# An attention and mixture-of-experts layer in float32: its products in two of 64 stationary columns each, and the scores' masked quarter left out

## The chip, the cores and the metric

The kernel runs on one core of a Trainium2 chip. The metric is the device time of one execution in microseconds (us); lower is better. Engines are named as in the profile: PE is TensorE's matmuls, PEld its weight loads, DVE is VectorE, ACT ScalarE, POOL GpSimd, SP the sync engine, whose queue issues nearly all DMA transfers.

## What is computed

The input is normalised, and three things are added to it: a linear attention with decay (32 heads of 128, 2 sequences of 512 tokens), and a base layer with eight low-rank experts, of which two are taken for each token. The attention is

```
qkv = silu(hidden_states @ qkv_w.T)
...
def step(kv, blk):
    cq, ck, cv = blk
    scores = jnp.einsum('bhnd,bhmd->bhnm', cq, ck) * diag_decay
    intra = jnp.einsum('bhnm,bhmd->bhnd', scores, cv)
    inter = jnp.einsum('bhnd,bhde->bhne', cq * q_decay, kv)
    kv_next = kv * block_decay + jnp.einsum('bhnd,bhne->bhde', ck * k_decay, cv)
    return (kv_next, intra + inter)
...
xf = xf * jax.lax.rsqrt(jnp.mean(xf * xf, axis=-1, keepdims=True) + EPS)
normed = norm_w * xf
gate = jax.nn.sigmoid(hidden_states @ gate_w.T)
return gate * normed @ out_w.T
```

`diag_decay` is zero where a key is later than the query, so within a block the scores are needed only where the key is not later. The reference uses blocks of 32 tokens; the kernel uses blocks of 128, which gives the same sum.

## The kernel before

Everything is float32. A product of a 128x128 stationary operand with N moving columns is one `nc.tensor.matmul` in the code, and two loads and two matmul records (here called passes) in the trace.

**Projections.** The products with the weights of v, gate, q and k are done by a fast scheme with seven products instead of eight, used twice, one inside the other. The list `rounds` has one entry for each outer product of each of 16 sets of weights; a round has seven slots (`SLOTS`), one for each inner product (`inner_product`, two products of 256 moving columns; L431 where tokens are stationary, which gives v, and L434 where the weights are). GpSimd forms the weights' sums two rounds ahead (`encode`, L162 to L187). `after` takes the results from PSUM with ScalarE and VectorE and adds them up. Sets 0 to 7 give v and gate, which go to DRAM; sets 8 to 15 give q and k of four heads each, which stay in SBUF.

**Attention.** As soon as q and k of one head and sequence (an item, 64 in all) are there, `attend` runs on it, in steps that are spread over the slots of later rounds by `stages` and `later`:

- v comes back from DRAM (L660).
- k's first three blocks are transposed: VectorE turns 32x32 squares (L665), a trip through DRAM puts the squares in their places (L668, then four transfers at L673) as `kt`.
- scores: four products of 128 keys (stationary) by 128 queries (L678), into one PSUM bank; VectorE multiplies them by the decays within a block (L680, `mask[:, 0]`), with keys on the partitions, into `sc`.
- GpSimd multiplies q by the decay from the block's start (L683, `mask[:, 1]`), the gate comes from DRAM (L686).
- ScalarE scales `kt` by each key's decay to the block's end into `kd` (L690), a column of the mask.
- three products of `kd` and v (L696), from which VectorE forms the running states (L698, L700).
- seven products (L706, L708) give the attention's output, transposed; VectorE multiplies it by the gate (L710), ScalarE squares it (L717), GpSimd adds the squares up (L718), and it goes to DRAM (L720).

`load_mask` (L446, L447) fetches an item's decays when the first part of its q and k is placed, four buffers in all: a 128x128 table with the keys on the partitions, and one row of 128 for the queries, given to all partitions.

**The rest.** The setup normalises x and transposes it on TensorE (L264, with an identity matrix), and runs the router and part of the base layer's products (L314). The output projection (`out_product`, L806) is again in seven products of 256 columns and begins before the attention ends.

**Order.** The order on PE, ACT, DVE, POOL and SP is the one in which the code issues the instructions (`tc.manual_schedule`). `mm` is a helper, so in the trace all its products have line 90. The tile tags tell them apart: `ps_sc<-qk` scores, `ps_sc<-v,kd` keys by values, `ps_at<-scores,v` and `ps_at<-qd,state` the output.

The "scores" ring has three buffers of 128x512. Before the attention it also serves the base layer's results and the experts' weights and biases.

Of the kernel before, what the change touches and what calls it, by code (L numbers as in the profile page):

```python
# [35 lines left out]
F32 = mybir.dt.float32  # L36
# [6 lines left out]
P = 128  # L43
# [18 lines left out]
def attn_moe_kernel(ctx: ExitStack, tc: tile.TileContext, x, qk_w, v_w, gate_w, out_w, norm_w,  # L62
# [22 lines left out]
    def ring(tag, shape=None):  # L85
        n, bufs = RING[tag]
        return work.tile(shape or [P, n * 512], F32, tag=tag, name=tag, bufs=bufs)

    def mm(o, lhsT, rhs, start, stop):
        nc.tensor.matmul(o, lhsT, rhs, start=start, stop=stop)  # L90

    ssq = [keep.tile([P, S], F32, tag=f"ssq{b}", name=f"ssq{b}") for b in range(B)]
    ident = keep.tile([P, P], F32, tag="ident", name="ident")
    nw = keep.tile([P, H], F32, tag="nw", name="nw")

    g_kept = [dram.tile([P, 2, 2, B, S // 2], F32, tag=f"g_kept{p}", name=f"g_kept{p}") for p in range(NP)]
# [108 lines left out]
    with tc.tile_pool(name="setup", bufs=1, side="right") as sp:  # L205
        x_sb = [sp.tile([P, HID], F32, tag=f"x{t}", name=f"x{t}") for t in range(NT)]
        nc.gpsimd.memset(eps, EPS)

        halves = (slice(0, HID // 2), slice(HID // 2, HID))
        for queue, of in zip((nc.sync, nc.scalar), halves):  # L210
# [76 lines left out]
        def base():  # L287

            pa, pb = seeded[:2], first_banks
            pc, pd, y, w = {}, {}, {}, {}  # L290

            def done(b, half, h, o):
                nc.sync.dma_start(x_base[:, TB * b + 2 * h : TB * b + 2 * h + 2, half * HO : (half + 1) * HO],
                                  o.rearrange("p (t n) -> p t n", t=2))

            def copied(tag, t):
                o = ring(tag, [P, 512])
                nc.scalar.copy(o, t)
                return o

            def added(t, u):
                o = ring("scores")
                nc.vector.tensor_tensor(o, t, u, ALU.add)
                return o


            units = [(1, 0, 0), (1, 0, 1), (2, 0, 0), (2, 0, 1), (1, 1, 0), (1, 1, 1), (2, 1, 0), (2, 1, 1)]
            for q, h, i in units + [(q, h, i) for q in (5, 6, 7, 3, 4) for h in range(2) for i in range(2)]:
                if q == 5 and i == 0:
                    pc[h] = bank("sc")  # L310
                t = {1: pa, 2: pa, 5: pc, 3: pc, 6: pb, 7: pd, 4: pd}[q][h]
                of = slice((2 * h + i) * P, (2 * h + i + 1) * P)
                for c in range(2):
                    nc.tensor.matmul(t[:, i * HO : (i + 1) * HO], xo[q][:, c, of], wo[q][:, c, :],  # L314
                                     start=q in (1, 5) and i == 0 and c == 0, stop=True, skip_group_check=True)
                if i == 0:
                    pass
                elif q == 1:
                    nc.scalar.copy(pb[h], t)
                elif q == 2:  # L320
                    done(0, 0, h, copied("scores", t))
                elif q == 5:
                    y[h] = copied("gT", t)
                elif q == 6:
                    pd[h] = pa[h]
                    nc.scalar.copy(pd[h], t)
                    w[h] = copied("gate", t)
                elif q == 7:
                    done(1, 1, h, added(t, y[h]))
                elif q == 3:  # L330
                    done(1, 0, h, added(t, w[h]))
                else:
                    done(0, 1, h, copied("scores", t))
                yield
# [16 lines left out]
        for g, ts in enumerate(groups):  # L351
            rstd = inv_sqrt(*roots[g])
            xns = []
            for i, t in enumerate(ts):
                xn = ring("gate")
                for of in halves if t == 0 else (slice(0, HID),):
                    (nc.vector if t < NT - 1 else nc.gpsimd).tensor_scalar(
                        xn[:, of], x_sb[t][:, of], mv[:, t, 0:1], rstd[:, i : i + 1], ALU.subtract, ALU.mult)
                xns.append(xn)

            for t in range(2 * g, 2 * g + 2) if 0 < g < 4 else ():
                statistics(t)
            for t, xn in zip(ts, xns):
                transpose(t, xn)
                for what in AFTER[t]:
                    if what == "base":
                        next(chunks)
                    else:
                        router(what)
        nc.vector.tensor_tensor(wsums[0], a21, a22, ALU.add)  # L370
        nc.vector.tensor_tensor(wsums[1], wsums[0], a11, ALU.subtract)
        nc.vector.tensor_tensor(wsums[2], a11, a21, ALU.subtract)
# [50 lines left out]
    def inner_product(o, r, i, first):  # L423
        n, q = rounds[r]
        a = operand[n, q][i]
        x_ = {1: xo[q][:, 0, :HB], 2: xo[q][:, 1, :HB], 3: xo[q][:, 1, HB:], 4: xt[q - 1][:, 3],
              5: xt[q - 1][:, 0], 6: xt[q - 1][:, 1], 7: xt[q - 1][:, 2]}[i]
        for u in range(2):
            if kind(n) == 0:

                nc.tensor.matmul(o.rearrange("p (g j d) -> p j g d", g=2, j=2)[:, u], x_[:, u * P : (u + 1) * P],  # L431
                                 a, start=first and u == 0, stop=True, skip_group_check=True)
            else:
                nc.tensor.matmul(o[:, u * HB : (u + 1) * HB], a[:, u], x_, start=first and u == 0, stop=True,  # L434
                                 skip_group_check=True)

# [3 lines left out]

    def load_mask(head):

        mask = work.tile([P, 2, P], F32, tag="mask", name="mask", bufs=4)
        nc.sync.dma_start(mask[:, 0, :], decay[head][:, :P])  # L446
        nc.sync.dma_start(mask[:, 1, :], decay[head][P - 1, P : 2 * P].partition_broadcast(P))  # L447
        return mask

    spare = cycle(5 * ["v"] + 2 * ["gT"])  # L450

# [202 lines left out]
    def attend(head, b):  # L654
# [7 lines left out]


        squares = work.tile([P, 4, TB - 1, 32], F32, tag="squares", name="squares", bufs=2)
        nc.vector.transpose(squares.rearrange("p c j d -> p j c d"), k[:, : (TB - 1) * P])  # L665
        yield
        kept = dram.tile([P, 4, TB - 1, 32], F32, tag="k_kept", name="k_kept", bufs=3)
        nc.sync.dma_start(kept, squares)  # L668
# [6 lines left out]

        pc = bank("sc")
        for j in range(TB):
            mm(pc[:, j * P : (j + 1) * P], k[:, j * P : (j + 1) * P], q[:, j * P : (j + 1) * P], True, True)  # L678
        sc = ring("scores", [P, TB, P])
        nc.vector.tensor_tensor(sc, pc.rearrange("p (j n) -> p j n", j=TB),  # L680
                                mask[:, 0, :].unsqueeze(1).to_broadcast([P, TB, P]), ALU.mult)
        qd = work.tile([P, TB - 1, P], F32, tag="qd", name="qd", bufs=3)
        nc.gpsimd.tensor_tensor(qd, q[:, P:].rearrange("p (j n) -> p j n", j=TB - 1),  # L683
                                mask[:, 1, :].unsqueeze(1).to_broadcast([P, TB - 1, P]), ALU.mult)
        gate = ring("gate")
        nc.sync.dma_start(gate, gate_kept[s_][:, u, f, b, :])  # L686
        yield

        kd = work.tile([P, TB - 1, P], F32, tag="kd", name="kd", bufs=2)
        nc.scalar.activation(kd.rearrange("p j (a d) -> p a j d", a=4), kt, AF.Copy,  # L690
                             scale=mask[:, 0, P - 1 : P])
        yield

        pu = bank("sc")
# [8 lines left out]
        pa = bank("at")  # L703
        for j in range(TB):
            o = pa[:, j * P : (j + 1) * P]
            mm(o, v[:, j * P : (j + 1) * P], sc[:, j, :], True, j == 0)  # L706
            if j:
                mm(o, state[:, j - 1, :], qd[:, j - 1, :], False, True)  # L708
        gT = ring("gT")
# [84 lines left out]
    def out_product(f, p, n, sums, only=None):  # L794

        a, w = gated[f, p], w_o[p]
        o = sums[n] if isinstance(sums[n], list) else [sums[n][:, i * HO : (i + 1) * HO] for i in range(2)]
        if n in (1, 2):
            l, r = a[:, n - 1, 0], w[:, n - 1, :HO]
        else:  # L800
            s, t = gsum[f, p], wsum[f, p]
            l, r = {3: (s[:, 3], w[:, 1, HO:]), 4: (a[:, 1, 1], t[:, 3]), 5: (s[:, 0], t[:, 0]),
                    6: (s[:, 1], t[:, 1]), 7: (s[:, 2], t[:, 2])}[n]
        for i in range(2):
            if only in (None, i):
                nc.tensor.matmul(o[i], l[:, i * P : (i + 1) * P], r,  # L806
                                 start=p == 0 and (i == 0 or isinstance(sums[n], list)), stop=p == NP - 1, skip_group_check=True)

    EARLY = 4
    sums = [{}, {}]  # L810
# [36 lines left out]
    for k in range(7 * len(rounds) + 7):  # L847
        now[0] = k
        r0, m = divmod(k, 7)
        if m == 0:  # L850
            if r0 == 3:
                routing = route()
            if r0 == 15:
                for slots, g in zip((2, 5, 11, 18), 4 * [transpose_experts()]):
                    later[k + slots].append(g)
            if r0 in range(18, 18 + 3 * NT, 3):
                for slots, g in zip((0, 8, 11, 13), 4 * [experts((r0 - 18) // 3)]):
                    later[k + slots].append(g)
# [257 lines left out]
```

## Time and profile before

| | us |
|---|---|
| median of 3 runs | 1130.0 (1128.63 to 1130.0) |
| span of the profiled execution | 1129.5 |
| granted TensorE clock | 1.00 throughout |
| DMA moved | 198.24 MB in 192254 packets, 176 GB/s |

The costliest groups of the attention and of the projections, by line, with busy time and the mean of one:

| line | what | count | busy us | mean ns |
|---|---|---|---|---|
| L434 | PE, `sd<-xt,e`, 256 columns (the largest such group) | 672 | 172.6 | 379 |
| L90 | PE, scores, 128 columns | 512 | 67.5 | 275 |
| L90 | PE, `kd` by v, 128 columns | 384 | 53.6 | 276 |
| L90 | PE, output from scores, 128 columns | 512 | 88.4 | 275 |
| L90 | PE, output from states, 128 columns | 384 | 74.2 | 275 |
| L680 | DVE, scores by decays, 128x512 | 64 | 43.9 | 686 |
| L665 | DVE, transposes of k, 128x384 | 64 | 35.6 | 566 |
| L690 | ACT, `kd`, 128x384 | 64 | 39.1 | 612 |
| L698 | DVE, copy from PSUM, 128x128 | 64 | 18.3 | 286 |
| L276 | ACT, copy from PSUM, 128x136 | 8 | 2.2 | 272 |

Matmuls are pipelined and their ends are modelled, so the mean of a PE record (379 ns) is longer than the distance from one to the next; the distance is read from the chain of waits in order of time, where a row is a start, a duration, and how many records follow each other. A count of PE records is a count of passes, two for each product. `SPq` is the queue of the sync engine; a row of a tile's view gives shortest, median and longest duration in ns, and then the first and last start in us.

### The profile page before, as it was taken

What the parts mean: (1) busy time and instruction counts of PE and PEld (TensorE: products, weight loads), DVE (VectorE), ACT (ScalarE), POOL (GpSimd) and SP (SyncE); (2) the same over time, 40 slices, a digit from 0 to 9 for tenths busy, and PEclk for the clock granted to TensorE, in tenths of its full rate; (3) what the DMA queues carried; (4) which work ended last, traced back from release to release, by engine and by line L of the source; (5) the groups of instructions that cost most, each with busy time, mean ns of one, the idle gap of its engine ahead of it and who ended that gap; (6) DMA issues with size and microseconds to landing.
All of it is one profiled execution on the core that took longest, in us unless ns stands there. A gap on an engine that the chain in (4) does not pass through costs nothing.

```text
span 1129.5 us, 18355 instructions
## 1 busy us (share of the span) xinstructions
PE 1120.4 (99%) x6064; PEld 1004.9 (89%) x6064; DVE 755.1 (67%) x1343; ACT 433.9 (38%) x778; POOL 763.5 (68%) x819
## 2 busy tenths in 40 slices
PE   8999999999999999999999999999999999999998
PEld 8888888888888888998999999999999998888887
DVE  7676766675665667776767767677777775545424
ACT  4344444444435434343343444435344442320000
POOL 3568778779768767666686866768776666554552
PEclk9999999999999999999999999999999999999999
DMA  5534574664553456666665766766666677943221
GB/s 169 161 112 158 168 235 157 193 203 156 186 168 122 159 146 198 168 195 187 208 193 173 209 170 179 204 190 198 179 186 174 200 229 242 329 162 118 90 92 56
DMA packets 192254, 198.24 MB, mean 176 GB/s; under 512 B 50976, under 2 KB 164384, under 8 KB 192032
## 3 DMA queue, kind: packets, MB, share of 16 engines
q1 hardware_dynamic: 192016, 196.94, 56.9%
q8 instruction: 49, 0.80, 0.3%
q14 instruction: 45, 0.37, 0.1%
q10 hardware_dynamic: 144, 0.13, 0.0%
HBM read 126.70 MB, written 70.30 MB: 174 GB/s over the span
## 4 chain that ended last, share of the span: by engine, by line
PE 93%; DMA 3%; DVE 2%; SPq 1%; issue 1%; POOL 1%; ACT 0%; ACTq 0%; DVEq 0%; POOLq 0%
PE ps_fr L434 20%; PE sd L434 18%; PE ps_at L90 9%; PE ps_sc L90 9%; PE sd L431 6%; PE sd L806 6%; PE ps_sc L806 5%; PE ps_fr L806 5%; PE ps_sc L434 4%; PE ps_sc L431 4%; PE ps_fr L431 4%; DMA k_kept<-squares 2%; PE ps_at L806 1%; PE sd L314 1%; DMA kt<-k_kept 1%; PE ps_sc L314 1%
## 5 line engine op out<-in xcount | busy, mean ns | idle before, releaser
L718 POOL TENSOR_TENSOR ssq<-ssq,sq 128x512 f32<-128x512 f32 x62 | 78.9, 1273 | 146.9 <-ACT sq L717 146.9
L434 PE MATMUL sd<-xt,e 128*128 128x256 f32 x672 | 172.6, 379 | 0.0
L483 ACT ACTIVATE qk<-qk 128x512 f32<-128x512 f32 x128 | 80.4, 630 | 207.0 <-DVE qk L506 206.9
L434 PEld LDWEIGHTS sd<-xt,e 128*128 128x128 f32 x672 | 123.6, 190 | 17.2 <-issue 2.6
L538 ACT COPY sd<-sd 128x512 f32<-128x512 f32 x112 | 64.1, 573 | 137.9 <-PE sd L434 69.3
L521 DVE TENSOR_TENSOR w<-sd,sum 128x512 f32<-128x512 f32 x110 | 74.5, 690 | 63.1 <-ACT sd L538 62.9
L527 ACT COPY sd<-ps_fr 128x512 f32<-128x512 f32 x112 | 64.2, 573 | 77.3 <-PE ps_fr L434 49.2
L90 PE MATMUL ps_at<-scores,v 128*128 128x128 f32 x512 | 88.4, 275 | 0.0
L787 POOL TENSOR_TENSOR wsum<-wo 128x256 f32<-128x256 f32 x48 | 39.2, 834 | 68.2 <-PE sd L806 28.9
L90 PEld LDWEIGHTS ps_at<-scores,v 128*128 128x128 f32 x512 | 77.4, 191 | 3.4
L786 DVE TENSOR_TENSOR gsum<-gated 128x256 f32<-128x256 f32 x54 | 25.9, 520 | 80.7 <-PE ps_sc L806 56.6
L162 POOL TENSOR_TENSOR s<-raw 128x1024 f32<-128x1024 f32 x32 | 75.6, 2364 | 5.0 <-DMA raw<-in_v_w 2.9
L90 PE MATMUL ps_at<-qd,state 128*128 128x128 f32 x384 | 74.2, 275 | 0.0
L434 PE MATMUL ps_fr<-xsum,s 128*128 128x256 f32 x288 | 74.0, 379 | 0.0
L710 DVE SCALAR_TENSOR_TENSOR gT<-gate,ps_at 128x512 f32<-128x512 f32 x64 | 43.6, 682 | 41.9 <-PE ps_at L90 36.8
L90 PEld LDWEIGHTS ps_sc<-qk 128*128 128x128 f32 x512 | 67.2, 192 | 3.3
L90 PE MATMUL ps_sc<-qk 128*128 128x128 f32 x512 | 67.5, 275 | 0.0
L181 POOL TENSOR_TENSOR e<-s 128x256 f32<-128x256 f32 x64 | 46.6, 728 | 28.7 <-PE sd L434 18.0
L683 POOL TENSOR_TENSOR qd<-qk,mask 128x384 f32<-128x384 f32 x64 | 64.3, 1005 | 2.4 <-PE ps_at L90 2.0
L680 DVE TENSOR_TENSOR scores<-ps_sc,mask 128x512 f32<-128x512 f32 x64 | 43.9, 686 | 22.4 <-PE ps_sc L90 20.0
L434 PEld LDWEIGHTS ps_fr<-xsum,s 128*128 128x128 f32 x288 | 53.1, 190 | 6.4
L90 PEld LDWEIGHTS ps_sc<-v,kd 128*128 128x128 f32 x384 | 52.6, 191 | 6.8 <-ACT kd L690 3.7
(345 smaller groups left out, 2905.8 us busy)
## 6 DMA issues: line engine op xcount, KB each, us to landing
raw<-in_qk_w SPq DMA_DIRECT2D x64, 256.0 KB, 4.3
v<-v_kept SPq DMA_DIRECT2D x64, 256.0 KB, 4.4
gate<-gate_kept SPq DMA_DIRECT2D x64, 256.0 KB, 3.3
g_kept<-gT SPq DMA_DIRECT2D x64, 256.0 KB, 3.3
gated<-g_kept SPq DMA_DIRECT2D x27, 512.0 KB, 3.8
k_kept<-squares SPq DMA_DIRECT2D x64, 192.0 KB, 3.5
kt<-k_kept SPq DMA_DIRECT2D x256, 48.0 KB, 2.1
gate_kept<-v SPq DMA_DIRECT2D x47, 256.0 KB, 2.5
```

What stands on the lines that cost most here:

```text
L90: nc.tensor.matmul(o, lhsT, rhs, start=start, stop=stop)
L162: nc.gpsimd.tensor_tensor(t, a, b, op)
L181: nc.gpsimd.tensor_tensor(e[:, 0], a21, a22, ALU.add)
L431: nc.tensor.matmul(o.rearrange("p (g j d) -> p j g d", g=2, j=2)[:, u], x_[:, u * P : (u + 1) * P], a, start=first and u == 0, stop=True, ...
L434: nc.tensor.matmul(o[:, u * HB : (u + 1) * HB], a[:, u], x_, start=first and u == 0, stop=True, skip_group_check=True)
L483: nc.scalar.activation(v, v, AF.Silu)
L521: nc.vector.tensor_tensor(o, v, t, ALU.add)
L527: nc.scalar.copy(st["pb"], st["pa"])
L538: nc.scalar.copy(st["pd"], st["pb"])
L683: nc.gpsimd.tensor_tensor(qd, q[:, P:].rearrange("p (j n) -> p j n", j=TB - 1), mask[:, 1, :].unsqueeze(1).to_broadcast([P, TB - 1, P]), A ...
L718: nc.gpsimd.tensor_tensor(ssq[b], ssq[b], sq, ALU.add)
L806: nc.tensor.matmul(o[i], l[:, i * P : (i + 1) * P], r, start=p == 0 and (i == 0 or isinstance(sums[n], list)), stop=p == NP - 1, skip_grou ...
```

## The change

A product in `mm`, once the setup's transposes are issued (`in_halves`), becomes two, each of 64 of the 128 stationary columns and all the moving columns; each writes its own 64 partitions of the result. `inner_product`, `out_product` and the base layer's products go through `mm` too. With `turned`, the two halves of the stationary columns change places in the result: this is done for the odd blocks of v, so that in an odd block tokens 64 to 127 stand on partitions 0 to 63.

The scores of a block become two products: the early 64 keys by all 128 queries, and the late 64 keys by the late 64 queries. The late keys by the early queries, which the decay makes zero, are no longer computed; their places in the three tiles of scores are set to zero once (`zero_scores`, at round 50), and the three tiles are then used in turn. In odd blocks the two products write the other half's partitions, as v's tokens stand there.

What follows from the order of the halves: the mask has five parts of 64 columns, loaded by five transfers (table and row, with halves exchanged for odd blocks). VectorE's multiplication of the scores becomes three instructions, one for the late queries of all blocks and two of 64 partitions for the early ones. The transposition of k becomes two, for the even blocks and for block 1, and the scaling to `kd` becomes two on ScalarE. The identity matrix moves to the setup's memory.

```diff
@@ -86,11 +86,20 @@
         n, bufs = RING[tag]
         return work.tile(shape or [P, n * 512], F32, tag=tag, name=tag, bufs=bufs)
-    def mm(o, lhsT, rhs, start, stop):
-        nc.tensor.matmul(o, lhsT, rhs, start=start, stop=stop)
+    HP = P // 2
+    in_halves = [False]
+    def mm(o, lhsT, rhs, start, stop, turned=0, **more):
+        if not in_halves[0]:
+            nc.tensor.matmul(o, lhsT, rhs, start=start, stop=stop, **more)
+            return
+        for h in range(2):
+            of = h ^ turned
+            nc.tensor.matmul(o[h * HP : (h + 1) * HP], lhsT[:, of * HP : (of + 1) * HP], rhs, start=start, stop=stop,
+                             **more)
     ssq = [keep.tile([P, S], F32, tag=f"ssq{b}", name=f"ssq{b}") for b in range(B)]
-    ident = keep.tile([P, P], F32, tag="ident", name="ident")
     nw = keep.tile([P, H], F32, tag="nw", name="nw")
     g_kept = [dram.tile([P, 2, 2, B, S // 2], F32, tag=f"g_kept{p}", name=f"g_kept{p}") for p in range(NP)]
@@ -205,6 +214,7 @@
     with tc.tile_pool(name="setup", bufs=1, side="right") as sp:
         x_sb = [sp.tile([P, HID], F32, tag=f"x{t}", name=f"x{t}") for t in range(NT)]
         nc.gpsimd.memset(eps, EPS)
+        ident = sp.tile([P, P], F32, tag="ident", name="ident")
         halves = (slice(0, HID // 2), slice(HID // 2, HID))
         for queue, of in zip((nc.sync, nc.scalar), halves):
@@ -311,8 +321,8 @@
                 t = {1: pa, 2: pa, 5: pc, 3: pc, 6: pb, 7: pd, 4: pd}[q][h]
                 of = slice((2 * h + i) * P, (2 * h + i + 1) * P)
                 for c in range(2):
-                    nc.tensor.matmul(t[:, i * HO : (i + 1) * HO], xo[q][:, c, of], wo[q][:, c, :],
-                                     start=q in (1, 5) and i == 0 and c == 0, stop=True, skip_group_check=True)
+                    mm(t[:, i * HO : (i + 1) * HO], xo[q][:, c, of], wo[q][:, c, :],
+                       q in (1, 5) and i == 0 and c == 0, True, skip_group_check=True)
                 if i == 0:
                     pass
                 elif q == 1:
@@ -367,6 +377,7 @@
                         next(chunks)
                     else:
                         router(what)
+        in_halves[0] = True
         nc.vector.tensor_tensor(wsums[0], a21, a22, ALU.add)
         nc.vector.tensor_tensor(wsums[1], wsums[0], a11, ALU.subtract)
         nc.vector.tensor_tensor(wsums[2], a11, a21, ALU.subtract)
@@ -428,11 +439,10 @@
         for u in range(2):
             if kind(n) == 0:
-                nc.tensor.matmul(o.rearrange("p (g j d) -> p j g d", g=2, j=2)[:, u], x_[:, u * P : (u + 1) * P],
-                                 a, start=first and u == 0, stop=True, skip_group_check=True)
+                mm(o.rearrange("p (g j d) -> p j g d", g=2, j=2)[:, u], x_[:, u * P : (u + 1) * P], a,
+                   first and u == 0, True, turned=u, skip_group_check=True)
             else:
-                nc.tensor.matmul(o[:, u * HB : (u + 1) * HB], a[:, u], x_, start=first and u == 0, stop=True,
-                                 skip_group_check=True)
+                mm(o[:, u * HB : (u + 1) * HB], a[:, u], x_, first and u == 0, True, skip_group_check=True)
@@ -442,10 +452,23 @@
     def load_mask(head):
-        mask = work.tile([P, 2, P], F32, tag="mask", name="mask", bufs=4)
-        nc.sync.dma_start(mask[:, 0, :], decay[head][:, :P])
-        nc.sync.dma_start(mask[:, 1, :], decay[head][P - 1, P : 2 * P].partition_broadcast(P))
+        mask = work.tile([P, 5, HP], F32, tag="mask", name="mask", bufs=4)
+        near = decay[head][:HP]
+        nc.sync.dma_start(mask[:HP, 0:2, :], near[:, :P])
+        nc.sync.dma_start(mask[:HP, 2, :], near[:, :HP])
+        nc.sync.dma_start(mask[HP:, 0, :], near[:, :HP])
+        nc.sync.dma_start(mask[HP:, 1:3, :], near[:, :P])
+        nc.sync.dma_start(mask[:, 3:5, :], decay[head][P - 1, P : 2 * P].partition_broadcast(P))
         return mask
+    score_tiles = []
+    def zero_scores():
+        for _ in range(RING["scores"][1]):
+            sc = ring("scores", [P, TB // 2, 2, 2, HP])
+            nc.gpsimd.memset(sc[HP:, :, 0, 0, :], 0.0)
+            nc.gpsimd.memset(sc[:HP, :, 1, 0, :], 0.0)
+            score_tiles.append(sc)
     spare = cycle(5 * ["v"] + 2 * ["gT"])
@@ -662,7 +685,10 @@
         squares = work.tile([P, 4, TB - 1, 32], F32, tag="squares", name="squares", bufs=2)
-        nc.vector.transpose(squares.rearrange("p c j d -> p j c d"), k[:, : (TB - 1) * P])
+        blocks_of_k = k.rearrange("p (j c d) -> p j c d", j=TB, d=32)
+        nc.vector.transpose(squares[:, :, 0::2].rearrange("p c j d -> p j c d"), blocks_of_k[:, 0 : TB - 1 : 2])
+        nc.vector.transpose(squares[:, :, 1].rearrange("p (h c) d -> p h c d", h=2)[:, ::-1],
+                            blocks_of_k[:, 1].rearrange("p (h c) d -> p h c d", h=2))
         yield
         kept = dram.tile([P, 4, TB - 1, 32], F32, tag="k_kept", name="k_kept", bufs=3)
         nc.sync.dma_start(kept, squares)
@@ -675,20 +701,32 @@
         pc = bank("sc")
         for j in range(TB):
-            mm(pc[:, j * P : (j + 1) * P], k[:, j * P : (j + 1) * P], q[:, j * P : (j + 1) * P], True, True)
-        sc = ring("scores", [P, TB, P])
-        nc.vector.tensor_tensor(sc, pc.rearrange("p (j n) -> p j n", j=TB),
-                                mask[:, 0, :].unsqueeze(1).to_broadcast([P, TB, P]), ALU.mult)
+            for late in range(2):
+                at, asked = late ^ (j % 2), slice(j * P + late * HP, (j + 1) * P)
+                keys = slice(j * P + late * HP, j * P + (late + 1) * HP)
+                nc.tensor.matmul(pc[at * HP : (at + 1) * HP, asked], k[:, keys], q[:, asked], start=True, stop=True,
+                                 skip_group_check=True)
+        sc = score_tiles[0]
+        score_tiles.append(score_tiles.pop(0))
+        scored = pc.rearrange("p (a r h n) -> p a r h n", a=TB // 2, r=2, h=2)
+        nc.vector.tensor_tensor(sc[:, :, :, 1], scored[:, :, :, 1],
+                                mask[:, 1:3].unsqueeze(1).to_broadcast([P, TB // 2, 2, HP]), ALU.mult)
+        for r in range(2):
+            of = slice(r * HP, (r + 1) * HP)
+            nc.vector.tensor_tensor(sc[of, :, r, 0], scored[of, :, r, 0],
+                                    mask[of, 0].unsqueeze(1).to_broadcast([HP, TB // 2, HP]), ALU.mult)
         qd = work.tile([P, TB - 1, P], F32, tag="qd", name="qd", bufs=3)
         nc.gpsimd.tensor_tensor(qd, q[:, P:].rearrange("p (j n) -> p j n", j=TB - 1),
-                                mask[:, 1, :].unsqueeze(1).to_broadcast([P, TB - 1, P]), ALU.mult)
+                                mask[:, 3:5].rearrange("p h n -> p (h n)").unsqueeze(1).to_broadcast([P, TB - 1, P]),
+                                ALU.mult)
         gate = ring("gate")
         nc.sync.dma_start(gate, gate_kept[s_][:, u, f, b, :])
         yield
         kd = work.tile([P, TB - 1, P], F32, tag="kd", name="kd", bufs=2)
-        nc.scalar.activation(kd.rearrange("p j (a d) -> p a j d", a=4), kt, AF.Copy,
-                             scale=mask[:, 0, P - 1 : P])
+        for r, js in enumerate((slice(0, TB - 1, 2), slice(1, 2))):
+            nc.scalar.activation(kd[:, js].rearrange("p j (a d) -> p a j d", a=4), kt[:, :, js], AF.Copy,
+                                 scale=mask[:, 1 + r, HP - 1 : HP])
         yield
         pu = bank("sc")
@@ -703,7 +741,7 @@
         pa = bank("at")
         for j in range(TB):
             o = pa[:, j * P : (j + 1) * P]
-            mm(o, v[:, j * P : (j + 1) * P], sc[:, j, :], True, j == 0)
+            mm(o, v[:, j * P : (j + 1) * P], sc[:, j // 2, j % 2].rearrange("p h n -> p (h n)"), True, j == 0)
             if j:
                 mm(o, state[:, j - 1, :], qd[:, j - 1, :], False, True)
         gT = ring("gT")
@@ -803,8 +841,8 @@
                     6: (s[:, 1], t[:, 1]), 7: (s[:, 2], t[:, 2])}[n]
         for i in range(2):
             if only in (None, i):
-                nc.tensor.matmul(o[i], l[:, i * P : (i + 1) * P], r,
-                                 start=p == 0 and (i == 0 or isinstance(sums[n], list)), stop=p == NP - 1, skip_group_check=True)
+                mm(o[i], l[:, i * P : (i + 1) * P], r, p == 0 and (i == 0 or isinstance(sums[n], list)), p == NP - 1,
+                   skip_group_check=True)
     EARLY = 4
     sums = [{}, {}]
@@ -853,6 +891,8 @@
             if r0 == 15:
                 for slots, g in zip((2, 5, 11, 18), 4 * [transpose_experts()]):
                     later[k + slots].append(g)
+            if r0 == 50:
+                zero_scores()
             if r0 in range(18, 18 + 3 * NT, 3):
                 for slots, g in zip((0, 8, 11, 13), 4 * [experts((r0 - 18) // 3)]):
                     later[k + slots].append(g)
```

## The prediction

> **What bounds the kernel now.** I read the page's totals first, then the table of stages, then the chain of waits in order of time.
>
> ```profile
> span 1129.5 us, 18355 instructions
> ## 1 busy us (share of the span) xinstructions
> PE 1120.4 (99%) x6064; PEld 1004.9 (89%) x6064; DVE 755.1 (67%) x1343; ACT 433.9 (38%) x778; POOL 763.5 (68%) x819
> ```
>
> TensorE fills 99% of the span, so a microsecond of its passes is a microsecond of time, unless something makes it wait. The attention items run from 400 to 940 us. There the stage table shows what room the others have:
>
> ```profile
> core 0: us, PE busy (x) PEld busy (x) DVE busy (x) ACT busy (x) POOL busy (x), PEclk, DMA share, GB/s
> 400.00:940.00 540.00, 538.29 (x3339) 495.89 (x3338) 393.27 (x720) 227.60 (x406) 377.96 (x387) 1.00 0.66 191
> ```
>
> TensorE misses 1.7 of 540 us at a granted clock of 1.00; VectorE is busy 73%. A busy record says little of what a pass costs; the chain gives its pace. Each float32 product stands there as two passes: the scores' four products as x8, the three of keys and values as x6, seven output products as x14.
>
> ```profile
> 646.05 0.89 PE ps_sc L90 x8
> 646.94 0.87 PE sd L434 x4
> 647.81 0.86 PE ps_fr L434 x4
> 648.67 0.67 PE ps_sc L90 x6
> 649.34 0.86 PE sd L434 x4
> 650.21 0.86 PE ps_fr L434 x4
> 651.07 1.56 PE ps_at L90 x14
> ```
>
> A pass of 128 moving columns costs 112 ns (0.89/8, 0.67/6, 1.56/14), one of 256 costs 216 ns (0.865/4). The timeline tells why 112 is over half of 216:
>
> ```profile
> 508.07 0.30 PEld L90 LDWEIGHTS ps_at<-qd,state 128*128 128x128 f32 x2
> 508.18 0.39 PE L90 MATMUL ps_at<-qd,state 128*128 128x128 f32 x2
> 508.30 0.73 PEld L434 LDWEIGHTS ps_fr<-xsum,raw 128*128 128x128 f32 x4
> 508.41 1.03 PE L434 MATMUL ps_fr<-xsum,raw 128*128 128x256 f32 x4
> ...
> 509.06 0.84 PEld L434 LDWEIGHTS ps_fr<-xt,e 128*128 128x128 f32 x4
> 509.27 1.03 PE L434 MATMUL ps_fr<-xt,e 128*128 128x256 f32 x4
> ```
>
> The weight load begins 0.11 us before its pass where passes have 128 columns, so load and pass are of one length there; beside 256 columns it has half the time to spare.
>
> **The sum, part by part.** It is made against the profiled execution, 1129.5 us, 0.5 below the median of the runs.
>
> *Scores.* An item has 8 passes of 128 columns: 8 x 112 = 896 ns. After, four blocks give 8 passes of 128 columns and 8 of 64, each on half of the stationary columns. If the two halves are worked side by side, each with its own order, the exchange in odd blocks gives either half 4 of 128 and 4 of 64. No row has 64 columns: half of 112 is 56, the line through 112 and 216 gives 60; I take 60, the dearer. 4 x 112 + 4 x 60 = 688, 208 ns saved, times 64 items: **-13.3 us**. Bounds: -14.3 (56 ns), and nothing.
>
> *All other products in two.* If the halves run beside each other, a slot of 216 or 112 ns carries two passes as it carried one, but two loads. If a load of 64 columns takes half of 112 ns, two take what one took: 0. If it took the whole 112, every slot would be at least 224: 1792 attention passes (64 x 28) lose 112 ns and the other 4272 lose 8, 201 + 34 = 235 us, the upper bound. Below: if loads of the two halves overlap, attention's passes come down to half of 216, 4 ns x 1792 = -7 us. I take **0**. The nearest fact is that one load fills 128 columns in 0.11 us; no row here loads fewer.
>
> The Trainium skill (TensorE: Matmul & The Clock Gate, "LDWEIGHTS") lets a load's time go with its columns; by that the zero stands. The trace, with 128 columns everywhere, cannot show it.
>
> *VectorE.* The scores' multiplication, 691 ns for 512 columns, becomes one of 256 and two of 128 on half the partitions. Copies from PSUM of 128 columns take 286 ns (L698); the line through 286 and 691 gives 421 for 256. 421 + 2 x 286 = 993, +0.30 us. The transposition of 384 columns (566 ns) becomes two; the same line's fixed part, 0.15 us, is paid once more. 64 x 0.45 = 29 us: 393 becomes 422 of 540, 78%. The cover is VectorE's own idle time; without it the 29 us would stand in the time.
>
> *ScalarE.* The scaling of kd (607 ns) in two: at most another 0.27 (the copy of 136 columns in setup, L276), 17 us on 228 of 540. Hidden. *GpSimd:* six memsets before the first item, each below the 0.73 us of a 128x256 operation: under 4.4 us, in a stage where it waits 2 to 4 us at a time for TensorE. Hidden. One switch to halves, the moved identity and the views: nothing.
>
> *SP's queue.* The mask comes in five transfers for two, 192 more on the one queue:
>
> ```profile
> L446 SPq DMA_DIRECT2D mask<-in_decay x64: 357/568/975, 403.3 to 922.6; - x64
> L447 SPq DMA_DIRECT2D mask<-in_decay x64: 333/448/1325, 404.0 to 923.2; - x64
> L673 SPq DMA_DIRECT2D kt<-k_kept x256: 302/424/1994, 411.1 to 935.9; - x128
> ```
>
> At 0.45 to 0.57 us that is 86 to 109 us of issuing. The stage now has some 704 issues (256 kt, 128 masks, 64 each of v, gate, g_kept, k_kept, q/k weights) at about 0.45: 317 of 540 us, 59%; then 75 to 79%. Behind the masks on that queue stand kt, v, gate, the stores and the next weights. What is late next is kt, then ScalarE's kd, then the products of keys and values:
>
> ```profile
>   DMA kt<-k_kept: 9.5, 5
> who waited for it (us, times):
>   ACT kd L690: 9.5, 5
>   PEld ps_sc L90: 3.7, 4
>   DVE gT L710: 2.3, 4
>   PE ps_sc L90: 2.2, 3
> ```
>
> TensorE and its loads lose up to 5.9 us on this path today. Bounds for the growth: 0 (the spare 40% of the queue takes it), and 86 us (all of it shows). As the queue keeps a fifth of its time, I take two thirds of today's loss again: **+4 us**, VectorE's later releases included.
>
> Sum: 1129.5 - 13.3 + 0 + 4 = 1120.2; with the half microsecond to the median, **1120.7 us**. Its own range: 1129.5 - 14.3 - 7 = 1108 to 1128 (gain as taken, three times the drag).
>
> **Rivals.** *Passes start strictly in order (slower).* The two passes of a product's first half come ahead of those of its second, so the second half then always lags by a pass. At equal lengths nothing is lost. But on going from 256 columns to 128, the first half is done while the other is still in its last long pass, and the next pass in the order belongs to that other half: one 128-column slot stays empty, 112 ns. The scores gain nothing either: a 64-column pass must wait its turn behind a 128-column pass of the other half, and two blocks take the eight slots that they took. The chain shows three such groups per item, each between 256-column products: 3 x 64 x 112 ns = 21.5 us, so 1129.5 + 21.5 + 4 = **1155**. It decides as soon as a pass that waits for its half holds back those behind it. For it: in the trace one pass follows another without exception. Against: with one tile of 128 columns nothing else could be seen, and TensorE does not work its records one by one (a load runs beside the pass ahead of it), so I give independent halves more than this.
>
> The Trainium skill speaks on both sides. TensorE: Matmul & The Clock Gate ("What overlaps and what doesn't") has matmuls in strict first-in, first-out order; TensorEngine Tiling (Array Packing) ("Key Properties") says that "Tiles operate independently". By the first the sum would be 1155, by the second 1121; no row of this case has two tiles.
>
> *SP or VectorE becomes late (slower or even).* A third of the 86 us showing gives +29 - 13 = 1145; a sixth leaves 1130. For it: SP waits its turn behind in-order waits, 77 us for k_kept alone. Against: those waits shrink when the queue is late.
>
> *The halves do not share the array.* Then passes are not overlapped, or loads stop them. Every slot at 224 gives 1365; no overlap at all adds nearly the 1100 us behind the transposes, some **2200**. The change would then not do what it says. Nothing in the profile excludes it.
>
> **How the numbers follow.** Independent halves with a small drag: 0.48. Strict order: 0.27. Late queue: 0.12, half of it within the band. Halves not shared: 0.08. Gains and losses nearly cancel for other reasons: 0.05 (0.01 faster, 0.01 within, 0.03 slower). Faster by over 0.2% (what a measurement can tell): 0.49; within: 0.07; slower: 0.44. The time is the likeliest case's, 1121. The range goes down to 1106 (every gain bound met, and the half-length passes) and up to 1165 (strict order with loads in sequence, 10 us more); 0.08 lies beyond from unshared halves and some 0.1 at both ends together.
>
> **What would show it.** Score products in the chain near 0.69 us an item; 256-column products still 0.86 to 0.87 for two; records of two halves overlapping in time; VectorE near 785 us; the wait of kd for kt below 20 us. Against it: score groups of 0.9 us or more and an extra 0.1 us at each entry into 128-column products mean strict order; 256-column products above 0.9 us mean loads; TensorE idle behind kt or v means SP.

## The result, and the profile after

The changed kernel takes 1179.1 us (median of 4, 1175.83 to 1180.17) against 1129.3 us; the ratio is 1.0436, with a 95% interval of 1.0423 to 1.0448. It is slower by some 50 us, where 8 less were forecast. The profiled execution, from its page:

```profile
span 1174.0 us, 30768 instructions
...
PE 1126.4 (96%) x11984; PEld 859.3 (73%) x11984; DVE 765.1 (65%) x1535; ACT 443.7 (38%) x842; POOL 764.4 (65%) x825
```

Twice as many passes are recorded, and TensorE is busy 96% instead of 99%. The stage of the attention (columns as in the prediction's stage table) shows where it stands still:

```profile
400.00:940.00 540.00, 507.54 (x6236) 394.03 (x6234) 383.38 (x855) 224.55 (x444) 356.80 (x363) 0.97 0.61 179
```

32 of 540 us are idle (1.7 before), and the granted clock is 0.97 instead of 1.00. Over the whole span it is 0.984. The products themselves did what was hoped. TensorE's timeline (start, duration, x passes):

```profile
642.74 1.06 PE L99 MATMUL ps_fr<-b,s 128*64 128x256 f32 x8
643.61 0.87 PE L707 MATMUL ps_sc<-qk 128*64 128x128 f32 x16
644.27 1.06 PE L99 MATMUL sd<-xt,e 128*64 128x256 f32 x8
645.14 0.85 PE L99 MATMUL ps_sc<-v,kd 128*64 128x128 f32 x12
```

From start to start the scores take 0.66 us (0.89 before); two products of 256 columns still take 0.87, now in 8 passes of halves. What TensorE waits for stands in the view of the tile kt (us, times):

```profile
  DMA kt<-k_kept: 50.1, 15
who waited for it (us, times):
...
  PEld ps_sc L99: 41.7, 13
  PE ps_sc L99: 35.8, 12
```

ScalarE waits 50.1 us for kt (9.5 before), TensorE 35.8 us for kd (2.2 before). One such wait, first on SP's queue, then on the engines:

```profile
651.71 0.57 SPq L457 DMA_DIRECT2D mask<-in_decay  x1
...
654.25 0.58 SPq L461 DMA_DIRECT2D mask<-in_decay  x1
...
657.72 0.86 SPq L694 DMA_DIRECT2D k_kept<-squares  x2
...
659.32 0.82 SPq L457 DMA_DIRECT2D mask<-in_decay  x1
...
662.73 1.86 SPq L699 DMA_DIRECT2D kt<-k_kept  x4
```

```profile
666.63 0.80 ACT L728 ACTIVATE kd<-kt,mask 128x256 f32<-128x256 f32 x2 [4.41 <-DMA kt<-k_kept]
...
667.20 1.02 PE L99 MATMUL ps_sc<-v,kd 128*64 128x128 f32 x10 [3.61 <-ACT kd L728]
```

Five mask transfers, 659.32 to 662.7, stand between the store of k's squares and the loads that bring it back. The same place in the kernel before:

```profile
637.25 0.80 SPq L668 DMA_DIRECT2D k_kept<-squares  x2
...
641.68 1.75 SPq L673 DMA_DIRECT2D kt<-k_kept  x4
```

From store to load it took 4.4 us there and takes 5.0 now, so most of the delay lies ahead of the store. VectorE had the squares of these two items ready at 652.25 and 652.77 us; SP, which issues without a break here, came to their stores only at 657.72 and 658.19, since five masks of another item (651.71 to 654.83), a gate and two v loads came first. In the kernel before, the stores went out 0.03 us after their squares. The same stretch of the changed kernel by windows shows a second loss behind the wait:

```profile
663.20:667.20 4.00, 0.39 (x5) 0.01 (x1) 1.39 (x3) 0.56 (x2) 3.92 (x6) 1.00 0.58 145
667.20:671.20 4.00, 4.00 (x28) 2.62 (x30) 1.23 (x4) 1.33 (x3) 0.17 (x1) 0.57 0.86 274
```

TensorE is idle for 3.6 us and then, busy again, gets a mean clock of 0.57: most of these 4 us run at half speed.

### The profile page after: what moved, and what is told of

Same layout as the page of the kernel before. It is cut to its first block, busy times and chain, and to the rows that moved or that the text cites. A ratio compares the mean times of both kernels' runs of the same rounds, so it can differ in the third digit from the quotient of the medians.

```text
span 1174.0 us, 30768 instructions
## 1 busy us (share of the span) xinstructions
PE 1126.4 (96%) x11984; PEld 859.3 (73%) x11984; DVE 765.1 (65%) x1535; ACT 443.7 (38%) x842; POOL 764.4 (65%) x825
## 4 chain that ended last, share of the span: by engine, by line
PE 62%; DMA 10%; DVE 8%; SPq 6%; POOL 6%; issue 5%; ACT 2%; DVEq 0%; ACTq 0%; POOLq 0%
PE sd L99 22%; PE ps_fr L99 18%; PE ps_sc L99 15%; PE ps_at L99 5%; DMA mask<-in_decay 4%; DMA k_kept<-squares 2%; DMA kt<-k_kept 2%; SPq L699 2%; DVE sum L529 1%; PE ps_sc L707 1%; DVE qk L529 1%; POOL ssq L756 1%; POOL qd L719 1%; POOL s L171 1%; SPq L458 1%
## 5 line engine op out<-in xcount | busy, mean ns | idle before, releaser
L99 PE MATMUL sd<-xt,e 128*64 128x256 f32 x1344 | 180.5, 387 | 0.0
L99 PEld LDWEIGHTS sd<-xt,e 128*64 128x64 f32 x1344 | 104.4, 140 | 36.4 <-issue 4.3
L99 PE MATMUL ps_at<-scores,v 128*64 128x128 f32 x1024 | 92.8, 281 | 0.0
L99 PE MATMUL ps_sc<-v,kd 128*64 128x128 f32 x768 | 56.5, 283 | 35.8 <-ACT kd L728 35.8
L99 PEld LDWEIGHTS ps_sc<-v,kd 128*64 128x64 f32 x768 | 46.8, 140 | 49.6 <-ACT kd L728 41.7
L99 PEld LDWEIGHTS ps_at<-scores,v 128*64 128x64 f32 x1024 | 68.8, 143 | 10.6 <-issue 2.8
L99 PE MATMUL ps_at<-qd,state 128*64 128x128 f32 x768 | 76.3, 276 | 0.0
L99 PE MATMUL ps_fr<-xsum,s 128*64 128x256 f32 x576 | 75.0, 379 | 0.0
L728 ACT ACTIVATE kd<-kt,mask 128x256 f32<-128x256 f32 (+1 forms) x128 | 50.9, 448 | 50.2 <-DMA kt<-k_kept 50.1
L707 PEld LDWEIGHTS ps_sc<-qk 128*64 128x64 f32 x1024 | 53.7, 137 | 8.6
```

The lines of the kernel that those rows point to most:

```text
L99: nc.tensor.matmul(o[h * HP : (h + 1) * HP], lhsT[:, of * HP : (of + 1) * HP], rhs, start=start, stop=stop, **more)
L707: nc.tensor.matmul(pc[at * HP : (at + 1) * HP, asked], k[:, keys], q[:, asked], start=True, stop=True, skip_group_check=True)
L728: nc.scalar.activation(kd[:, js].rearrange("p j (a d) -> p a j d", a=4), kt[:, :, js], AF.Copy, scale=mask[:, 1 + r, HP - 1 : HP])
```

## The experiments

Eleven kernels ran, each timed beside the kernel before. The table has medians and ratios to before with their intervals; the theories are named in the expectations.

| run | us | ratio |
|---|---|---|
| one_mask | 1126.9 | 0.9973 (0.9953 to 0.9993) |
| before_five | 1169.7 | 1.0352 (1.0332 to 1.0371) |
| halves_only | 1142.6 | 1.0117 (1.0090 to 1.0144) |
| masks_act | 1197.2 | 1.0604 (1.0585 to 1.0623) |
| one_mask_v | 1117.8 | 0.9897 (0.9877 to 0.9916) |
| halves_v | 1125.3 | 0.9961 (0.9948 to 0.9974) |
| before_v | 1129.2 | 1.0002 (0.9992 to 1.0012) |
| split_only | 1129.4 | 1.0003 (0.9993 to 1.0013) |
| after_v | 1171.9 | 1.0388 (1.0360 to 1.0416) |
| no_exchange | 1126.1 | 0.9975 (0.9964 to 0.9986) |
| scores_in_halves | 1136.4 | 1.0063 (1.0048 to 1.0078) |

**One transfer a mask.** The five parts lie together in DRAM.

```diff
-        near = decay[head][:HP]
-        nc.sync.dma_start(mask[:HP, 0:2, :], near[:, :P])
...
-        nc.sync.dma_start(mask[:, 3:5, :], decay[head][P - 1, P : 2 * P].partition_broadcast(P))
+        nc.sync.dma_start(mask, decay[head])
```

> The changed kernel, but the five parts of a mask lie together in DRAM (laid out with the other constants) and come in one transfer: 256 transfers fewer than the change, 64 fewer than before; everything else of the change stays. Theory Q (the 192 added transfers overload SP's queue, kt comes late, TensorE waits for kd, and the waits lower its clock): the 41.7 us of waits for kd shrink to a few us, no half-speed stretches, and the time is before - 14.7 (scores) - 5 (attention passes at 109 instead of 112 ns) with up to 4 of drag: 1109 to 1116. Rival V (the split instructions on VectorE and ScalarE make kd and the banks late): 1160 or more, the waits stay. Rival P (the halved products themselves cost it): 1150 or more, with TensorE busy all the time.

1126.9 us: 52 us of the changed kernel's time go, but the result lies between the theories' numbers. TensorE still waits 6.9 us for kd. The mask transfers are the largest cause, and not the only one.

**The old kernel with five transfers a mask.**

```diff
-        nc.sync.dma_start(mask[:, 0, :], decay[head][:, :P])
+        for i in range(2):
+            for j in range(2):
+                of, at = slice(i * P // 2, (i + 1) * P // 2), slice(j * P // 2, (j + 1) * P // 2)
+                nc.sync.dma_start(mask[of, 0, at], decay[head][of, at])
```

> The kernel before, with the 128x128 table of the mask in four transfers of 64x64 (five transfers a mask instead of two, 384 rows as in the change); no product, no VectorE or ScalarE instruction is touched. Theory Q: 1129 plus the 50 to 70 us that the change lost, 1175 to 1200, with waits for kd of 40 us or more and half-speed stretches; somewhat less if the faster products of the change made the queue tighter: not under 1150. Rivals V and P: 1129 to 1133.

1169.7 us: 40 us lost with no product changed, a little less than theory Q's 1175 to 1200. The view of kt has the same signature, and TensorE's waits are smaller than the 40 us expected:

```profile
  DMA kt<-k_kept: 43.6, 14
...
  PE ps_sc L90: 23.3, 11
```

**The halved products alone.** `mm`, `inner_product`, `out_product` and the base layer as in the change; all else as before.

> The kernel before, with every product behind the transposes in two of 64 columns, and nothing else of the change: whole scores, the old mask, no exchange. Theory Q: halves run side by side, 256-column passes at 216 ns, 128-column passes at 109 instead of 112: 1129 - 5 = 1122 to 1127. Rival P: slower than 1135. Strictly ordered passes (the prediction's first rival): 1129 + 21 = 1150.

1142.6 us, above every number of theory Q. Yet passes keep their pace: 0.87 us for the 16 passes of the scores, 0.86 for 8 of 256 columns. The loss is again waits for kd, 11.0 us on TensorE, and two half-speed stretches. What differs most clearly is the landing of the store of k's squares (last column, median us from issue), first before, then here:

```profile
k_kept<-squares SPq DMA_DIRECT2D x57, 192.0 KB, 3.5
```

```profile
k_kept<-squares SPq DMA_DIRECT2D x56, 192.0 KB, 4.2
```

In the timeline of SP's queue the two v loads (256 KB each) are issued at 636.98 and the stores at 637.89 us, right behind them; in the kernel before SP waits there for the squares, and the store goes out 1.4 us after the v loads. A longer landing keeps SP waiting for it (105.0 us in all, 77.1 before), with everything that stands behind. This led to theory L.

**The masks on ScalarE's queue.** In `load_mask`, `nc.sync` became `nc.scalar`.

> The changed kernel, its five mask transfers issued by ScalarE's queue instead of SP's; their number, sizes and rows stay. Theory Q (the time that SP needs to issue them): SP is back at its load of before, time 1110 to 1130, unless ScalarE (38% busy, 5 x 0.59 us more for each item, 189 us in all) becomes late itself. Rival T (not the issuing but the many short rows, or too many transfers under way, delay kt): the waits for kt stay and the time is 1160 or more.

1197.2 us, the slowest of all, but not by rival T: ScalarE's wait for kt falls from 50.1 to 1.3 us, though the transfers are the same. So it is their place on SP's queue, not the transfers as such, that made kt late; that it is the time of issuing is read from SP's timeline above, where one issue follows the other. (This kernel also stands still elsewhere, which gives kt more time.) On ScalarE the same burst blocks ScalarE:

```profile
ACT qk L506 <- DMA mask<-in_decay: 84.5, 24, 4.9
```

Behind the five issues wait the activation of q and k and the copies out of PSUM. TensorE then waits 49.3 us for the release of `ps_fr` banks by VectorE, itself behind those copies (VectorE's `w` waits 127.3 us for ScalarE's `sd`, 68.1 in the changed kernel).

**The v load behind the store of the squares**, on the changed kernel with one mask transfer, on the halves alone, and on the kernel before:

```diff
         v = ring("v")
-        nc.sync.dma_start(v, v_kept[s_][:, u, f, b, :])
-        yield
...
         nc.sync.dma_start(kept, squares)
         yield
+        nc.sync.dma_start(v, v_kept[s_][:, u, f, b, :])
+        yield
...
-        for slots in (1, 2, 3, 6):
+        for slots in (2, 3, 4, 6):
```

> The changed kernel with one transfer a mask, and each item's v load issued two steps later, behind the store of k's squares instead of ahead of it (slots 2, 3, 4, 6 instead of 1, 2, 3, 6). Theory L (what is left of the lost time is the round trip of k through DRAM, whose store lands late because the 256 KB v loads are just ahead of it on the queue): k_kept lands in 3 us or less instead of 4.2, waits for kd below 3 us, 1110 to 1118. Rival B (VectorE's and ScalarE's split instructions hold the banks, the 0.685 us waits before ps_fr): kd's waits may go, but 1122 or more stays.

> The kernel before with every product in two halves, nothing else of the change, and the v load moved behind the store of the squares. Theory L: the 11 us of kd waits and the half-speed stretches of the halves alone vanish: 1129 - 5 = 1122 to 1126. Rival P (the halved products cost time by themselves): stays at 1135 or more.

> The kernel before with only the v load moved behind the store of the squares: the control of the two runs above. Theory L: its own three kd waits (3.4 us) go, 1125 to 1130. If moving the load harms (v late for the products with kd): 1133 or more.

All three came in as theory L has it: 1117.8, 1125.3 and 1129.2 us. The store now lands sooner, here in one_mask_v:

```profile
k_kept<-squares SPq DMA_DIRECT2D x59, 192.0 KB, 2.6
```

ScalarE's waits for kt fall from 17.0 to 2.5 us. The move is worth 9 us with the change's products and one transfer, 17 us on the halves alone, and nothing on the kernel before: there too the store lands sooner (2.6 us, 3.5 before), but TensorE had only 2.2 us of waits for kd to lose. one_mask_v beats both kernels. Why the halves alone bring SP to the store just behind the v loads was not isolated.

**The split instructions alone**, on the kernel before: the scores' multiplication in three, the transposition and kd in two each.

> The kernel before with VectorE's score multiplication in three instructions (256, 128 and 128 columns), the transposition in two and kd's scaling in two, as in the change; products and transfers stay. Theory Q (SP's queue is what cost the time): 1129 to 1134, VectorE busy up by some 25 us. Rival V (the split instructions make the chain of kt late): 1140 or more.

1129.4 us, no difference. VectorE's busy time rises by 10 us, not 25 (755.1 to 764.8): rival V is out.

**The change with only the v load moved.**

> The changed kernel with its five mask transfers, and only the v load moved behind the store of k's squares. If the load on SP's queue by itself (83% of the stage spent issuing) keeps kt late: 1140 or more, kd waits over 15 us. If only the order of the transfers mattered, and five transfers are bearable in the better order: 1118 to 1125.

1171.9 us, kd waits 32.4 us: with five transfers a mask the better order gains some 7 of 50 us. The load on the queue is a cause by itself.

**Without the exchange.** Based on halves_v, with the late keys' scores for early queries left out in natural order:

```diff
-            mm(pc[:, j * P : (j + 1) * P], k[:, j * P : (j + 1) * P], q[:, j * P : (j + 1) * P], True, True)
+            for late in range(2):
+                asked = slice(j * P + late * HP, (j + 1) * P)
+                keys = slice(j * P + late * HP, j * P + (late + 1) * HP)
+                nc.tensor.matmul(pc[late * HP : (late + 1) * HP, asked], k[:, keys], q[:, asked], start=True, stop=True,
```

> Products in halves, v load moved, the old mask in two transfers; the late keys' scores for the early queries are left out, but the halves of odd blocks are not exchanged, so the first half of the columns has 128 columns in every block and the second 64. Theory (each half has its own order, and the fuller one sets the time): the scores stay at 8 x 109 = 0.87 us an item, 1122 to 1128, as with whole scores in halves. If leaving out is worth half its gain without the exchange: 1115 to 1121.

1126.1 us, as halves_v (1125.3). The chain, which doesn't follow every pass of halves, has the scores at 0.87 us:

```profile
649.99 0.87 PE ps_sc L698 x11
```

Leaving the quarter out is worth nothing while one half of the columns has all of its 128-column passes; the exchange is what turns it into time.

**Only the scores in halves.**

```diff
+            if r0 == 60:
+                in_halves[0] = False
```

> The version with one transfer a mask and the moved v load, but from round 60 on (q and k sets, attention, output) all products except the scores are whole again, so TensorE goes from whole to half columns and back once for each item. If such a switch costs nothing: 1118 plus 5 for the other attention passes at 112 ns, 1121 to 1125. If it has to run empty first (in the trace a pass's result is there 163 ns after the next one may start: 379 less 216), two switches an item cost up to 0.33 us, 21 us: up to 1146.

1136.4 us, within the costly branch. The chain, first of one_mask_v, then of this run:

```profile
647.71 0.66 PE ps_sc L702 x12
648.37 0.87 PE ps_fr L99 x8
```

```profile
646.94 0.81 PE ps_sc L702 x12
647.75 1.07 PE sd L95 x4
```

0.15 us more on the way in and 0.20 on the way out: 0.35 us an item, of the 0.40 by which its period is longer. A mix of whole and halved products eats the gain, which speaks for halving everything, as the change does.

## Why the prediction was wrong

**Scores: right.** 13.3 us were taken (0.69 us an item); 0.66 was measured, (0.89 - 0.66) x 64 = 14.7 us. The period of an item in the steady part of a set is 8.31 us before, 8.24 in halves, 8.03 with scores left out and exchanged: (8.24 - 8.03) x 64 = 13.4 us.

**Other products in two: right, a little better than the zero taken.** 128-column passes go from 112 to 109 ns a slot, near half of 216, as the prediction's lower bound has it; that the shorter loads are the reason was not isolated. halves_v against before is -3.7 us (1129.0 to 1125.3), between the bounds of -7 and +235.

**VectorE, ScalarE: right to cost nothing.** The time is unchanged in split_only; the 29 us of busy time were too many. In one_mask_v, once in each set of items, TensorE enters a product 0.47 us late, since ScalarE is still copying a `ps_fr` bank, 7 times, 3.3 us. It is part of why 7.5 us, not 13.4, lie between halves_v and one_mask_v. Neither split_only nor scores_in_halves has more than 0.3 us of such waits, so the split instructions alone don't make them; what does was not isolated.

**SP's queue: the step that failed.** It was put so: "As the queue keeps a fifth of its time, I take two thirds of today's loss again: +4 us". The mechanism was the named one, kt late, then kd, then the products of keys and values; its size was off by an order. Measured: 35.8 us of TensorE's waits, and a clock of 0.984, which over 1174 us is 19 us; together 55 of the 58 us between the changed kernel's span and one_mask_v's 1116.2.

Three things were missed. An issue of a mask part takes 0.59 us, not 0.45 to 0.57, so masks go from 65 us of SP's time (64 x 1.02) to 189 (64 x 2.96), 124 more instead of at most 109. A share of free time says nothing of a queue worked in order, on which k's squares go out and must come back: masks stand ahead of the store and between store and load, and what is free elsewhere doesn't help. And once in every set of eight items two items end together, so two of these round trips and their masks fall together; that is where most of the long waits are (2.6 to 4.6 us, some 72 us apart in the trace).

For the second item of these eight pairs the trace gives, on average, 4.8 us from the squares to the store's issue (0.6 before), 4.9 from there to the landing (4.7), and 3.4 from the landing to the load's issue (2.3): 13.0 us instead of 7.6, four fifths of the growth ahead of the store. The prediction's ground against a late queue, that SP's own waits shrink, came true (its wait for k_kept fell from 77.1 to 10.2 us) and did not help.

**The clock: left out.** Nothing in the sum let a wait cost more than itself; here that was the 19 us above.

**The rivals.** Strict order of passes (1155) fell: the scores take 0.66 us where it has 0.89, and in halves_only the groups of 128-column products take 0.87 and 0.66 us, without the extra 0.11 at their entry. Halves that do not share the array fell as well: 256-column passes of the two halves start by turns 35 and 181 ns apart, within the 216 ns that one took. The late queue was the right rival, with 0.12 and at 1145, a third of the 86 us; about two thirds of it showed, counting the clock. The range ended at 1165, below the time, since it stacked only the strict order's price.

## What to carry to other kernels

Count what an edit adds to a DMA queue as a load on everything behind it in the same order, above all when a tile goes out and comes back on that queue; look there for the longest round trip and for what stands ahead of it, not for the share of free time. A tile that needs rearranging costs less as one transfer from a layout made beforehand than as five. Halved stationary columns pay where their halves carry equal work, and if products around them are halved too.

## What the runs showed of the hardware

Two products of 64 stationary columns ran side by side, with their own orders: eight passes of 128 columns and eight of 64 took 0.66 us when spread evenly over both halves, and 0.87 when one half had all of the 128s. The Trainium skill (TensorE: Matmul & The Clock Gate, "The mechanism", under "What overlaps and what doesn't") states strict first-in, first-out order for matmuls; here equal totals on the two halves finished 0.21 us earlier than unequal ones, which one common order of starts, as the rival had it, does not give. So the measurement decides for TensorEngine Tiling (Array Packing), "Key Properties": tiles operate independently.

The same section says that changing the mode drains TensorE. The trace of scores_in_halves agrees: 0.15 and 0.20 us more at the two ends of each group of scores.

Long waits of TensorE came with a stretch of 3.4 us, sometimes 6.8, at half its clock. In the changed kernel there are ten waits of 2.3 to 5 us from pass to pass in 440 to 990 us, and nine such stretches, each beginning within 1.3 us of the end of one of them, 37.5 us in all; in one_mask_v, whose waits in the attention are 0.7 us at most, there is none. TensorE: Matmul & The Clock Gate ("HAM oscillation — how this bites in real kernels") has idle gaps over some 3.4 us as the trigger; in the changed kernel 2.3 us from pass to pass was enough at 982 us, and 3.0 us at 735 us had no effect, so the measurement decides: a wait shorter than the page's limit can be enough.

The time for SP to issue one transfer hardly depends on its size: a mask part of 16 KB took 0.59 us (median), the whole mask of 160 KB also 0.59 us in one_mask, and 0.43 in one_mask_v.
